# Three graph layers on one core: the first 112 nodes gathered edge by edge, or counted like all others

## The chip, the cores and the metric

The kernel runs on one core of a Trainium2 chip. The metric is the device time of one execution in microseconds (us), taken as the median of several runs. TensorE (PE) multiplies, VectorE (DVE) and ScalarE (ACT) work elementwise, GpSimd (POOL) does the same more slowly and issues transfers, SyncE (SP) only issues transfers.

## The reference

There are N = 2500 nodes with 256 numbers each and E = 80000 edges, sorted by destination. Three layers follow a normalization; a final product takes all four stages.

```python
h = jnp.maximum(_layernorm(x, axis=-1), 0.0)
def _edge_conv(x, src, dst, W, b):
    xi = x[dst]
    xj = x[src]
    m = jnp.concatenate([xi, xj - xi], axis=-1) @ W + b
    s = jax.ops.segment_sum(m, dst, num_segments=N)
    cnt = jax.ops.segment_sum(jnp.ones((dst.shape[0],), m.dtype), dst, num_segments=N)
    return s / jnp.maximum(cnt, 1.0)[:, None]
xs = [h]
for W, b in ((W0, b0), (W1, b1), (W2, b2)):
    h = jax.nn.relu(_edge_conv(h, src, dst, W, b))
    xs.append(h)
out = x + jnp.concatenate(xs, axis=-1) @ Wf + bf
```

A layer is linear before its Relu. With the halves Wt and Wb of W it is, up to the division by the in-degree, `cnt * h (Wt - Wb) + A (h Wb)`, where `A[d, s]` is the number of edges from s to d.

## The kernel before, in words

**Data.** The nodes are 20 tiles of 128 (`NT`, the last one with 68). `hT` holds the layer's input turned, features on the partitions and nodes in columns. `z` is `h Wb`, nodes on the partitions; it is split into two reduced-precision parts, `zh` and `zl`, so that two fast matmuls give the accuracy of one slow one.

**The count matrix.** Destinations are taken in windows of six nodes (`W`). For a window, up to 256 of its edges are fetched, and two one-hot tiles are made from source and destination by comparing on DVE (`compare`, which writes `one_m` and `one_n`); their product on PE (`counts`) is the window's part of the count matrix, which ACT takes out of the bank (`take_counts`). Four windows are a batch, 80 windows a group of 480 columns: groups 0 to 3 have 480, group 4 has 468. A group is a tile `a` of 20 source tiles by its columns.

**The first 112 nodes.** Windows begin at node 112 (`FEW`). The first 112 nodes have another way. `z` is kept in DRAM (`z_dram`: `keep_nodes` in layer 1, a store in `nodes_pair` later). For edge number e of each of these nodes, `gather` fetches the row of `z` of its source by an indirect transfer from POOL, 56 transfers a layer, eight of which fill eight slots of `sums` while the others add to them. `add_sums` adds the eight slots on DVE. `few_start` puts the own product of the 112 nodes into two PSUM banks on PE, and `few_end` adds the gathered sums by a product with `only`, a shifted identity, and takes the Relu.

**Layer 1** (`layer`, called for g = 0 to 4). For each group PE does 80 wide matmuls (20 source tiles, two output halves, `zh` and `zl`) and four own products, and in between, at seven points, the `counts` of the next group. `finish` completes a group (a row for the bias) and stores it to `a_dram` in bf16: POOL transfers that narrow on the way for groups 0 to 3; for group 4 `store_a` narrows on ACT and SP stores. On POOL's queue a part of the layer's gathers stands ahead of each store (`GATHERED`), and the five `add_x` transfers, which add x to the output, ahead of group 1's. What comes before the first group is an order written out by hand (`order`, a list of short names: C for `counts`, E for `take_counts`, B for `compare`, X and Y for the steps of `keep_nodes`, `ix` for `few_edges`).

**Layers 2 and 3.** `nodes_pair(l, t)` makes `z` for tiles t and t + 10, with their sums in `sh` and `sl`, and adds the previous layer's part of the final product (`final`). Then `Stream` runs the count matrix out of `a_dram`: `Alone` is group 4, by 80 wide matmuls; each `Pair` is two groups at once, by a scheme of seven products (`SEVEN`) in place of eight, 140 wide matmuls and seven own products. SP loads a chunk (`staged`, three buffers), ACT or DVE makes its `block`s five steps ahead (`LEAD`), PE multiplies. Since the gathers need all of `z` in DRAM, the work on the first nodes of the next layer is put late: the pair of tiles 0 and 10 comes after two steps of `Alone`, the chunk with tile 0 is the last one (`CHUNKS`), and the next layer's weights are loaded behind it. These lines set that order:

```python
        stream.run(tick, {0: [few_end], 2: [first_nodes], 12: [sums_of_w]})
    ts = [*range(1, 8), NT - 3, NT - 2, NT - 1, *range(8, NT - 3)]
```

All recorded instructions go through one helper, so the profile gives line 282 for nearly all of them; they are told apart by their tiles. The order on each engine is the program's own. At the end a flag (`missing`) says whether the counted edges are E; if they are not, a general version runs.

Of the kernel before, what the change touches and what calls it, by code (L numbers as in the profile page):

```python
# [313 lines left out]
def by_windows(ctx: ExitStack, tc: tile.TileContext, x, src, dst, Ws, bs, Wf, bf, out, missing):  # L314
# [17 lines left out]
    FEW = 112  # L332
    EDGES = 56
    SUMS = 8
    PAIRS = 4
    NW = (N - FEW) // W
# [3 lines left out]
    NONE = NP - 1  # L340
# [7 lines left out]
    while sum(GWS) < NW:  # L348
        GWS.append(min(80, NW - sum(GWS)))
    G = max(GWS) * W  # L350
    GS = 480
# [10 lines left out]
    assert E == P * R and FEW + NV == N and IN_LAST + FEW <= P and BW * NB <= 512 and G <= 512 and CAP <= 256  # L362
# [43 lines left out]
    z_dram = [dram.tile([NP, D], F32, name=f"z_dram{l}") for l in range(L)]  # L406
    who = const.tile([P, EDGES], I32, name="who")
    sums = const.tile([P, SUMS, D], F32, name="sums")
    only = const.tile([P, FEW], F32, name="only")
    cnt_few = const.tile([P, FEW], F32R, name="cnt_few")  # L410
    mine = const.tile([P, W], F32, name="mine")
    most = const.tile([P, 1], F32, name="most")
# [55 lines left out]
    POOLo.iota(lim_i[:, :WG - 1], pattern=[[P * W, WG - 1]], base=FEW, channel_multiplier=W)  # L468
    POOLo.iota(lim_i[:, WG - 1:], pattern=[[0, 1]], base=-IN_LAST, channel_multiplier=1)
    POOLo.iota(lim_i[:IN_LAST, WG - 1:], pattern=[[0, 1]], base=FEW + (WG - 1) * P * W, channel_multiplier=W)  # L470
    limr_i = pp.tile([P, WG * P], I32, name="limr_i")
    POOLo.iota(limr_i[:, :NW], pattern=[[W, NW]], base=FEW, channel_multiplier=0)
    POOLo.iota(limr_i[:, NW:], pattern=[[1, WG * P - NW]], base=0, channel_multiplier=0)
# [9 lines left out]
    def load_b(l, queue=SP):  # L483
# [8 lines left out]
    POOL.tensor_copy(only, ident[:, IN_LAST:IN_LAST + FEW])  # L492
    POOL.memset(cnt_few.bitcast(F32), 0.0)

    POOL.memset(mine, 0.0)
    POOL.affine_select(mine[:, 0:1], ones, pattern=[[0, 1]], compare_op=OP.is_ge, fill=0.0,
                       base=IN_LAST + FEW - 1, channel_multiplier=-1)
    POOL.memset(mine[:IN_LAST], 1.0)
    POOL.memset(most, float(EDGES))
    POOL.memset(most[:IN_LAST], float(CAP))  # L500
# [122 lines left out]
    def few_edges():  # L623

        es, ed = edges[WG - 1]
        own = pp.tile([P, EDGES], I32, name="own")
        POOLo.tensor_scalar(who, es[:, :EDGES], -NONE, None, op0=OP.add)
        POOLo.tensor_scalar(own, away[:, WG - 1, :EDGES], 1.0, None, op0=OP.is_equal)
        POOLo.tensor_tensor(who, who, own, op=OP.mult)
        POOLo.tensor_scalar(who, who, NONE, None, op0=OP.add)  # L630

# [28 lines left out]
    def degrees(i):  # L660
# [12 lines left out]
        for w0 in range(0, min(P, NW - i * P), P // 2):  # L673
            n = min(P // 2, NW - i * P - w0)
            pc = bank()
            for c in range(W):
                PEo.matmul(pc[:, :n * W].rearrange("p (w c) -> p w c", c=W)[:, :, c],
                          deg_b[:, i, c:c + 1].to_broadcast([P, P]), ident_b[:, w0:w0 + n], start=True, stop=True)
            to = FEW + (i * P + w0) * W
            ACTo.copy(cnt[:, to:to + n * W], pc[:, :n * W])  # L680
            yield
        if i == WG - 1:
            pc = bank()
            PEo.matmul(pc[:, :FEW], deg_b[:, i, 0:1].to_broadcast([P, P]), ident_b[:, IN_LAST:IN_LAST + FEW],
                       start=True, stop=True)
            ACTo.copy(cnt[:, :FEW], pc[:, :FEW])
            ACTo.copy(cnt_few[PAD:PAD + 1], cnt[PAD:PAD + 1, :FEW])
            yield

    def shares():  # L690
# [5 lines left out]
        last = deg[:, WG - 1, :]  # L696
        DVEo.scalar_tensor_tensor(last, last, most, mine, op0=OP.min, op1=OP.mult)
# [112 lines left out]
    def group_of(g):  # L810
        return FEW + sum(GWS[:g]) * W, GWS[g] * W
# [57 lines left out]
    def finish(g, a):  # L869
# [4 lines left out]
        gathered(GATHERED[g])  # L874
        if g == 1:
            for t in range(0, NT, 5):
                add_x(t, t + 5)
        store_a(g, a)
        yield

    def store_a(g, a):
        if g < alone:
            for t in range(0, NT, 5):
                POOLo.dma_start(a_dram[g][:, t:t + 5, :], a[:, t:t + 5, :].bitcast(F32))
            return
        short = new_a(g + 1).rearrange("p t n -> p (t n)").bitcast(BF16)[:, :NT * GS].rearrange(
            "p (t n) -> p t n", n=GS)
        for t in range(0, NT, 2):
            ACTo.copy(short[:, t:t + 2, :], a[:, t:t + 2, :].bitcast(F32))
        for t in range(0, NT, Q):  # L890
            SPo.dma_start(a_dram[g][:, t:t + Q, :], short[:, t:t + Q, :])

    def by_count(g):
        c0, n = group_of(g) if g < NG else (0, FEW)
# [3 lines left out]

    def keep_nodes(l, a, b):

        to = z_dram[l][a * P:b * P, :].rearrange("(q i p) d -> p i q d", i=2, p=P)
        ways = [(slice(0, 2), 0)] if b - a == 2 else [(i, slice(None)) for i in range(2)]

        def tiles_of(z):
            return z[:, :, a // 2 * D:b // 2 * D].bitcast(F32).rearrange("p i (q d) -> p i q d", d=D)

        for i, q in ways:
            SPo.dma_start(to[:, i, q, :], tiles_of(zh)[:, i, q, :])
        yield
        for i, q in ways:  # L910
            POOLo.dma_start(to[:, i, q, :], tiles_of(zl)[:, i, q, :], accum_op=OP.add)

    def gather(l):

        for e in range(EDGES):
            POOLo.indirect_dma_start(
                out=sums[:, e % SUMS, :], out_offset=None, in_=z_dram[l][:, :],
                in_offset=bass.IndirectOffsetOnAxis(ap=who[:, e:e + 1], axis=0),
                **({"compute_op": OP.add} if e >= SUMS else {}))
            yield  # L920

    first_gather = [None, 0]

    def gathered(n):
        if first_gather[0] is None:
            first_gather[0] = gather(0)
        while first_gather[1] < n:
            next(first_gather[0], None)
            first_gather[1] += 1

    few_banks = []

    def few_start(l):
        few_banks[:] = bank(), bank()
        for o, pa in enumerate(few_banks):
            for c in range(DC):
                PEo.matmul(pa[:, :FEW], ws[l][0][:, c, o * P:(o + 1) * P], hT[:, c, :FEW], start=(c == 0), stop=False)
            for z in (zh, zl):
                PEo.matmul(pa[:, :FEW], tile_of(z, NT - 1)[:, o * P:(o + 1) * P], cnt_few, start=False, stop=False)

    def add_sums():
        n = SUMS
        while n > 1:
            n //= 2
            DVEo.tensor_add(sums[:, :n, :], sums[:, :n, :], sums[:, n:2 * n, :])

    def few_end():
        for o, pa in enumerate(few_banks):
# [95 lines left out]
    for g in range(NG):  # L1044
# [12 lines left out]
        for u, _ in enumerate(layer(0, g, a, own, PEo, ACTo)):  # L1057
# [7 lines left out]
            if u == NT - 1 and g + 1 < NG:  # L1065
                run(extra)
                by_count(g + 1)
                if g == NG - 2:
                    by_count(NG)
# [319 lines left out]
```

## Time and profile before

| what | value |
|---|---|
| median of 3 runs | 520.09 us (519.41 to 520.48) |
| the profiled execution, its time | 520.36 us |
| its span, first to last instruction | 518.6 us |
| granted TensorE clock, mean | 0.962 |
| busy: PE, DVE, ACT, POOL | 478.4, 362.6, 244.8, 338.4 us |
| transfers | 82.42 MB, 159 GB/s |
| gathers (`sums<-z_dram,who`) | 168, 1672 ns each on POOL |

The span lies 1.76 us under the time of the same execution. Busy times of engines overlap. PE's busy time is modelled at the ends of matmuls, which are pipelined: a row of 0.37 us can be followed by the next one after 0.21 us, so steps are read from start to start. In rows of a timeline the columns are start, length, engine, line, operation, output and inputs with their shapes, count, and in brackets the idle time before it with what ended it.

### The profile page before, as it was taken

How to read it: one execution, taken by the hardware profiler on the slowest of the kernel's cores; microseconds unless marked ns; L12 is line 12 of the kernel's file. 1: busy time of each engine (PE TensorE's matmuls, PEld its weight loads, DVE VectorE, ACT ScalarE, POOL GpSimd, SP SyncE). 2: the span in 40 equal slices, each digit the busy share in tenths (PEclk: the TensorE clock that was granted, in tenths of full speed). 3: DMA queues.
4: the chain of work that ended last, by engine and by line, in shares of the span. 5: the costliest groups of instructions: out<-in, count | busy, mean ns of one | idle time of the engine just before them, and what ended most of it. 6: DMA issues, size and time to landing. Idle time of an engine off the chain costs nothing.

```text
span 518.6 us, 7749 instructions
## 1 busy us (share of the span) xinstructions
PE 478.4 (92%) x2787; PEld 393.0 (76%) x2787; DVE 362.6 (70%) x764; ACT 244.8 (47%) x458; POOL 338.4 (65%) x252
## 2 busy tenths in 40 slices
PE   8999999999999999989999999999599999999503
PEld 4878887788787887868888688788487877878402
DVE  7999889888988503586859688577534878865203
ACT  5667576846443543367454353357193444421000
POOL 4687338677888885000488888888007888888850
PEclk9999999999999999997999999999799999999856
DMA  9326995997988999933869887679377686846991
GB/s 292 123 83 121 184 218 147 185 210 108 181 132 149 134 191 164 194 119 106 293 172 212 200 197 144 116 129 168 57 213 258 144 228 118 197 60 123 159 79 49
DMA packets 60921, 82.42 MB, mean 159 GB/s; under 512 B 5337, under 2 KB 55978, under 8 KB 60586
## 3 DMA queue, kind: packets, MB, share of 16 engines
q0 software_dynamic: 30032, 38.62, 50.3%
q1 hardware_dynamic: 29914, 42.11, 25.7%
q10 hardware_dynamic: 928, 1.11, 0.7%
q8 instruction: 24, 0.39, 0.3%
q14 instruction: 23, 0.19, 0.1%
HBM read 56.48 MB, written 25.98 MB: 159 GB/s over the span
## 4 chain that ended last, share of the span: by engine, by line
POOL 37%; PE 34%; issue 11%; DMA 9%; DVE 6%; ACT 1%; SPq 0%; POOLq 0%; DVEq 0%; ACTq 0%
POOL sums L282 36%; PE bank L282 31%; DMA z_dram<-tmp 5%; PE pz L282 3%; DMA acc<-in_x_dram 1%; DMA sums<-z_dram,who 1%; DMA wb<-in_L_gnn_W_dram 1%; DVE sums L282 1%; DMA es<-in_src_dram,start_i 1%; DVE one_m L282 1%; DVE one_n L282 1%; POOL acc L282 1%; DVE tmp L282 1%; DVE zl L282 1%; ACT tmp L282 1%
## 5 line engine op out<-in xcount | busy, mean ns | idle before, releaser
L282 POOL DMA_INDIRECT sums<-z_dram,who x168 | 280.9, 1672 | 71.1 <-issue 47.5
L282 ACT CAST block<-staged 128x960 fp32r<-128x960 bf16 x80 | 74.5, 992 | 37.7 <-issue 22.7
L282 PE MATMUL bank<-block,zh 128*128 128x480 f32 (+1 forms) x200 | 84.1, 420 | 0.0
L282 PE MATMUL bank<-a,zh 128*128 128x480 f32 (+1 forms) x200 | 81.2, 406 | 0.0
L282 PE MATMUL bank<-block,zl 128*128 128x480 f32 (+1 forms) x200 | 77.8, 389 | 0.0
L282 DVE TENSOR_TENSOR one_m<-iota_m,key_m 128x1024 bf16<-128x1024 bf16 x100 | 68.5, 685 | 13.2 <-PE bank L282 12.3
L282 ACT CAST a<-bank 128x480 fp32r<-128x480 f32 x100 | 50.6, 566 | 55.2 <-PE bank L282 54.1
L282 PE MATMUL bank<-a,zl 128*128 128x480 f32 (+1 forms) x200 | 75.7, 378 | 0.0
L282 DVE TENSOR_TENSOR block<-block,staged 128x960 fp32r<-128x960 f32 x60 | 67.7, 1154 | 4.6 <-PE bank L282 1.7
L282 PE MATMUL bank<-block,sh 128*128 128x480 f32 x160 | 66.8, 417 | 0.0
L282 DVE TENSOR_TENSOR one_n<-iota_n,key_n 128x480 bf16<-128x480 bf16 x200 | 63.6, 357 | 0.0
L282 PE MATMUL bank<-block,sl 128*128 128x480 f32 x160 | 60.6, 379 | 0.0
L282 PE MATMUL bank<-wf,hT 128*128 128x256 f32 x240 | 56.7, 386 | 0.0
L282 PEld LDWEIGHTS bank<-wf,hT 128*128 128x128 f32 x240 | 46.4, 194 | 6.5
L282 PEld LDWEIGHTS bank<-block,zh 128*128 128x128 f32 x200 | 39.5, 198 | 8.4 <-issue 3.0
L282 PEld LDWEIGHTS bank<-block,zl 128*128 128x128 f32 x200 | 39.4, 197 | 8.3 <-issue 3.0
L282 PEld LDWEIGHTS <-one_m 128*128 128x128 bf16 x796 | 37.3, 98 | 9.0 <-issue 3.4
L282 PEld LDWEIGHTS bank<-a,zh 128*128 128x128 f32 x200 | 37.7, 188 | 8.2 <-issue 3.1
L282 PEld LDWEIGHTS bank<-a,zl 128*128 128x128 f32 x200 | 37.7, 188 | 6.9 <-issue 2.1
L282 PE MATMUL bank<-one_n,one_m 128*128 128x120 bf16 (+1 forms) x796 | 42.4, 208 | 0.1
L282 ACT ACTIVATE hT<-bank 128x480 f32<-128x480 f32 (+2 forms) x20 | 8.9, 482 | 65.3 <-PE bank L282 65.3
L282 POOL DMA_DIRECT2D z_dram<-tmp x2 | 1.6, 792 | 57.8 <-ACT tmp L282 57.8
(168 smaller groups left out, 706.8 us busy)
## 6 DMA issues: line engine op xcount, KB each, us to landing
staged<-a_dram SPq DMA_DIRECT2D x42, 480.0 KB, 5.7
a_dram<-a POOLq DMA_DIRECT2D x16, 600.0 KB, 12.5
z_dram<-tmp SPq DMA_DIRECT2D x18, 256.0 KB, 3.9
staged<-a_dram SPq DMA_DIRECT2D x16, 240.0 KB, 4.6
sums<-z_dram,who POOLq DMA_INDIRECT x168, 5.3
out_dram<-acc SPq DMA_DIRECT2D x19, 128.0 KB, 4.9
a_dram<-a SPq DMA_DIRECT2D x2, 1200.0 KB, 11.3
acc<-in_x_dram POOLq DMA_DIRECT2D x3, 640.0 KB, 9.7
```

The source lines that it names most:

```text
L282: return self.tc.keep_in_program_order(call(*args, **kwargs))
```

## The change

All nodes from 0 on go through windows: 417 windows (the last reaches two columns past node 2499), in groups of 84 windows or 504 columns, the last with 81 or 486. A group has 21 batches of four windows (the last group a final batch of one), where it had 20. `FEW` and all that served it is gone: the gathers, `who`, `sums`, the stores of `z` to DRAM, `few_start`, `add_sums`, `few_end`. Since no work waits for `z` in DRAM, the node pairs run in order (layer 3 begins with pair 6, then 0), all ahead of `Alone`, chunks are (0, 1), (2, 3) and so on, each loaded by two transfers, and the next layer's weights are loaded after the last node pair. Group 4 is stored by POOL like the others, and `add_x` follows the store of group 0. In the order by hand, one batch is added to group 0 (C20, E20, and B24 for the batch ahead). In the diff below, removed functions are cut to their first line, and small edits in setup are left out.

```diff
     SKIP = 2
-    FEW = 112
-    EDGES = 56
-    SUMS = 8
-    PAIRS = 4
-    NW = (N - FEW) // W
+    NW = -(-N // W)
     NV = NW * W
...
     IN_LAST = NW - (WG - 1) * P
-    NONE = NP - 1
     NB = NT * W
...
     while sum(GWS) < NW:
-        GWS.append(min(80, NW - sum(GWS)))
+        GWS.append(min(84, NW - sum(GWS)))
     G = max(GWS) * W
-    GS = 480
+    GS = G
     NG = len(GWS)
...
     const.tile([P, 16], F32, name="between")
-    z_dram = [dram.tile([NP, D], F32, name=f"z_dram{l}") for l in range(L)]
-    who = const.tile([P, EDGES], I32, name="who")
-    sums = const.tile([P, SUMS, D], F32, name="sums")
-    only = const.tile([P, FEW], F32, name="only")
-    cnt_few = const.tile([P, FEW], F32R, name="cnt_few")
-    mine = const.tile([P, W], F32, name="mine")
-    most = const.tile([P, 1], F32, name="most")
     pairs = [(0, 1), (2, 3)]
...
     POOL.tensor_copy(ident_b, ident)
-    POOL.tensor_copy(only, ident[:, IN_LAST:IN_LAST + FEW])
...
     warm = pp.tile([P, 1], F32, name="warm")
...
         parts[i] = [lo_i]
-    def few_edges():
...
                           deg_b[:, i, c:c + 1].to_broadcast([P, P]), ident_b[:, w0:w0 + n], start=True, stop=True)
-            to = FEW + (i * P + w0) * W
+            to = (i * P + w0) * W
             ACTo.copy(cnt[:, to:to + n * W], pc[:, :n * W])
-            yield
-        if i == WG - 1:
-            pc = bank()
-            PEo.matmul(pc[:, :FEW], deg_b[:, i, 0:1].to_broadcast([P, P]), ident_b[:, IN_LAST:IN_LAST + FEW],
-                       start=True, stop=True)
-            ACTo.copy(cnt[:, :FEW], pc[:, :FEW])
-            ACTo.copy(cnt_few[PAD:PAD + 1], cnt[PAD:PAD + 1, :FEW])
             yield
...
     def group_of(g):
-        return FEW + sum(GWS[:g]) * W, GWS[g] * W
+        return sum(GWS[:g]) * W, GWS[g] * W
...
         ACTo.copy(a[PAD:PAD + 1, NT - 1, :n], cnt[PAD:PAD + 1, c0:c0 + n])
-        gathered(GATHERED[g])
-        if g == 1:
+        for t in range(0, NT, 5):
+            POOLo.dma_start(a_dram[g][:, t:t + 5, :], a[:, t:t + 5, :].bitcast(F32))
+        if g == 0:
             for t in range(0, NT, 5):
                 add_x(t, t + 5)
-        store_a(g, a)
         yield
-    def store_a(g, a):
-        if g < alone:
-            for t in range(0, NT, 5):
-                POOLo.dma_start(a_dram[g][:, t:t + 5, :], a[:, t:t + 5, :].bitcast(F32))
-            return
-        short = new_a(g + 1).rearrange("p t n -> p (t n)").bitcast(BF16)[:, :NT * GS].rearrange(
-            "p (t n) -> p t n", n=GS)
-        for t in range(0, NT, 2):
-            ACTo.copy(short[:, t:t + 2, :], a[:, t:t + 2, :].bitcast(F32))
-        for t in range(0, NT, Q):
-            SPo.dma_start(a_dram[g][:, t:t + Q, :], short[:, t:t + Q, :])
     def by_count(g):
-        c0, n = group_of(g) if g < NG else (0, FEW)
+        c0, n = group_of(g)
         for o in range(DC):
...
-    def keep_nodes(l, a, b):
...
-    def gather(l):
...
-    def gathered(n):
...
-    def few_start(l):
...
-    def add_sums():
...
-    def few_end():
...
     a = new_a(0)
-    kept = [keep_nodes(0, i, j) for i, j in ((0, 4), (10, 16), (16, NT), (4, 8), (8, 10))]
     acts = {
...
         "se": lambda i: search(*((0, 1), (1, WG))[i]), "ge": get_edges,
-        "ix": few_edges, "ka": key_parts, "km": key_low, "kb": key_high, "kt": key_turn,
+        "ka": key_parts, "km": key_low, "kb": key_high, "kt": key_turn,
...
         k11 N8 L6 B4 E2 L5 C3 B5 C4 T8 E3 E4 C5 V9 R8 E5 ge3 ka2 H9 sc2 Z7 H7 F8 G7 B6 N3 N2 ka3 km2 T2 R2 km3
-        kb2 C6 T3 kb3 B7 L7 kt2 Z2 B8 B9 L9 X0 X1 E6 C7 k22 k12 kt3 H2 N4 ix Y0 Y1 E7 B10 k13 k23 Z8 L2 C8 T4 C9 E8
-        C10 H8 X2 E9
-        F9 B11 B12 C11 G8 E10 C12 R4 E12 E11 B13 F5 B14 C13 R3 B15 C14 E13 E14 L8 Y2 B16 Z3 G9 B17 C15 C16 H3 X3 E15
-        G5 B18 F3 C17 E16 C18 F4 E17 B19 C19 Z4 L3 Y3 G3 B20 E18 B21 F2 E19 B22 H4 X4 L4 Y4 G4 B23 G2 ws
+        kb2 C6 T3 kb3 B7 L7 kt2 Z2 B8 B9 L9 E6 C7 k22 k12 kt3 H2 N4 E7 B10 k13 k23 Z8 L2 C8 T4 C9 E8
+        C10 H8 E9
+        F9 B11 B12 C11 G8 E10 C12 R4 E12 E11 B13 F5 B14 C13 R3 B15 C14 E13 E14 L8 B16 Z3 G9 B17 C15 C16 H3 E15
+        G5 B18 F3 C17 E16 C18 F4 E17 B19 C19 Z4 L3 G3 B20 E18 C20 B21 F2 E19 B22 H4 E20 L4 G4 B23 G2 B24 ws
     """
...
     LATE = [NT] * 4
-    GATHERED = [0, 8, 21, 34, EDGES]
     extra = chain(degrees(0), finish(0, a), later_loads(), degrees(1))
...
                 by_count(g + 1)
-                if g == NG - 2:
-                    by_count(NG)
         run(extra)
...
                 ACTo.activation(zf[:, part], pz[:, part], AF.Copy, scale=share[:, u:u + 1])
-        (SPo if t else POOLo).dma_start(z_dram[l].rearrange("(h t p) d -> p h t d", h=2, p=P)[:, :, t, :],
-                      zf.rearrange("p (h d) -> p h d", h=2))
         ACTo.copy(both_of(zh, t), zf.rearrange("p (h d) -> p h d", h=2))
...
             st = stage.tile([P, 4, 2, GS], BF16, name="staged")
-            j0, j1 = CHUNKS[c]
-            for k, n in ((0, 2),) if j1 == j0 + 1 else ((0, 1), (1, 1)):
-                j = CHUNKS[c][k]
-                for i, g in enumerate(pairs[self.i]):
-                    SPo.dma_start(st[:, 2 * i:2 * i + 2, k:k + n, :],
-                                  a_dram[g].rearrange("p (h j) n -> p h j n", h=2)[:, :, j:j + n, :])
+            j = 2 * c
+            for i, g in enumerate(pairs[self.i]):
+                SPo.dma_start(st[:, 2 * i:2 * i + 2, :, :],
+                              a_dram[g].rearrange("p (h j) n -> p h j n", h=2)[:, :, j:j + 2, :])
             return st
...
             to = self.bank[what]
-            if c == len(CHUNKS) - 1:
+            if c == Q // 2 - 1:
                 if part[0] == "x":
...
                 PEo.matmul(to, w, self.r[what] if m is None else m, start=False, stop=False)
-            for k, j in enumerate(CHUNKS[c]):
+            for k, j in enumerate((2 * c, 2 * c + 1)):
                 for z in range(2):
...
                                          start=(c == 0 and k == 0 and z == 0),
-                                         stop=(c == len(CHUNKS) - 1 and k == 1 and z == 1))
+                                         stop=(c == Q // 2 - 1 and k == 1 and z == 1))
...
             n = self.n
-            if c == 1 and i == 0:
+            if c == 0 and i == 0:
                 self.banks = [bank(), bank()]
...
                         unit[0] = PEo.matmul(self.banks[o][:, :n], tile_of(z, t)[:, o * P:(o + 1) * P],
-                                             made[i][:, k, :n], start=(t == 4 and z is zh), stop=False)
-            if c == 0 and i == 1:
+                                             made[i][:, k, :n], start=(t == 0 and z is zh), stop=False)
+            if c == 4 and i == 1:
                 for o in range(DC):
...
         for p in Alone(l), Pair(l, 0), Pair(l, 1):
-            for c in range(5) if isinstance(p, Pair) else (1, 3, 4, 2, 0):
+            for c in range(5) if isinstance(p, Pair) else (0, 1, 3, 2, 4):
                 loads.append((p, c))
...
         stream.load(3)
-        order = [1, 2, 3, 4, 5, 6, 7, 8, 9] if l == 1 else [6, 7, 1, 2, 3, 4, 5, 8, 9]
-        for i, t in enumerate(order):
+        for i, t in enumerate(range(Q) if l == 1 else [6, 0, 1, 2, 3, 4, 5, 7, 8, 9]):
             nodes_pair(l, t)
-            if i == 0:
-                few_start(l - 1)
-            if i == 5:
+            if i == 6:
                 stream.make(2)
-            if i == 6:
-                add_sums()
-        def first_nodes():
-            nodes_pair(l, 0)
-            run(gather(l))
-            load_wf(l + 1, SPo)
-            if l + 1 < L:
-                load_b(l + 1, SPo)
-                load_wb(l + 1, SPo)
-                load_wt(l + 1, SPo)
+        load_wf(l + 1, SPo)
+        if l + 1 < L:
+            load_b(l + 1, SPo)
+            load_wb(l + 1, SPo)
+            load_wt(l + 1, SPo)
...
-        stream.run(tick, {0: [few_end], 2: [first_nodes], 12: [sums_of_w]})
+        stream.run(tick, {12: [sums_of_w]})
         if l + 1 < L:
...
-    ts = [*range(1, 8), NT - 3, NT - 2, NT - 1, *range(8, NT - 3)]
-    few_start(L - 1)
-    for i, t in enumerate(ts):
+    for t in [*range(7), NT - 4, NT - 3, NT - 2, NT - 1, *range(7, NT - 4)]:
         final(L, t)
-        if i == NT - 5:
-            add_sums()
-        if i == NT - 3:
-            few_end()
-    final(L, 0)
```

More of the change, by code (lines that the diff above doesn't have):

```diff
@@ L361, in by_windows @@
     assert NP <= 4096 and HR <= 512
-    assert E == P * R and FEW + NV == N and IN_LAST + FEW <= P and BW * NB <= 512 and G <= 512 and CAP <= 256
+    assert E == P * R and N <= NV <= NP and BW * NB <= 512 and G <= 512 and CAP <= 256
     assert E + P < 2 ** 24 and LAST <= PAD < P - 1 and D == DC * P
@@ L467, in by_windows @@
     lim_i = pp.tile([P, WG], I32, name="lim_i")
-    POOLo.iota(lim_i[:, :WG - 1], pattern=[[P * W, WG - 1]], base=FEW, channel_multiplier=W)
-    POOLo.iota(lim_i[:, WG - 1:], pattern=[[0, 1]], base=-IN_LAST, channel_multiplier=1)
-    POOLo.iota(lim_i[:IN_LAST, WG - 1:], pattern=[[0, 1]], base=FEW + (WG - 1) * P * W, channel_multiplier=W)
+    POOLo.iota(lim_i[:, :WG - 1], pattern=[[P * W, WG - 1]], base=0, channel_multiplier=W)
+    POOLo.iota(lim_i[:, WG - 1:], pattern=[[0, 1]], base=NP, channel_multiplier=0)
+    POOLo.iota(lim_i[:IN_LAST, WG - 1:], pattern=[[0, 1]], base=(WG - 1) * P * W, channel_multiplier=W)
     limr_i = pp.tile([P, WG * P], I32, name="limr_i")
-    POOLo.iota(limr_i[:, :NW], pattern=[[W, NW]], base=FEW, channel_multiplier=0)
-    POOLo.iota(limr_i[:, NW:], pattern=[[1, WG * P - NW]], base=0, channel_multiplier=0)
+    POOLo.iota(limr_i[:, :NW], pattern=[[W, NW]], base=0, channel_multiplier=0)
+    POOLo.iota(limr_i[:, NW:], pattern=[[0, WG * P - NW]], base=NP, channel_multiplier=0)
     row_i = pp.tile([P, MORE], I32, name="row_i")
@@ L491, in by_windows @@
     POOL.tensor_copy(ident_b, ident)
-    POOL.tensor_copy(only, ident[:, IN_LAST:IN_LAST + FEW])
[L493 to L500, printed above, removed]
     warm = pp.tile([P, 1], F32, name="warm")
@@ L621, in key_parts @@
         parts[i] = [lo_i]
-    def few_edges():
[L625 to L630, printed above, removed]
     def key_low(i):
@@ L694, in shares @@
         found = hot.tile([P, 1], F32, name="found")
-        last = deg[:, WG - 1, :]
-        DVEo.scalar_tensor_tensor(last, last, most, mine, op0=OP.min, op1=OP.mult)
         DVEo.reduce_sum(found, deg.rearrange("p i c -> p (i c)"), axis=mybir.AxisListType.X)
@@ L893, in by_count @@
     def by_count(g):
-        c0, n = group_of(g) if g < NG else (0, FEW)
+        c0, n = group_of(g)
         for o in range(DC):
             DVEo.tensor_mul(hT[:, o, c0:c0 + n], hT[:, o, c0:c0 + n], cnt[:, c0:c0 + n])
-    def keep_nodes(l, a, b):
[L901 to L911, printed above, removed]
@@ L913, in gather @@
-    def gather(l):
[L915 to L922, printed above, removed]
-    def gathered(n):
[L925 to L929, printed above, removed]
@@ L931, in by_windows @@
-    few_banks = []
-    def few_start(l):
[L934 to L939, printed above, removed]
-    def add_sums():
[L942 to L945, printed above, removed]
@@ L947, in few_end @@
-    def few_end():
-        for o, pa in enumerate(few_banks):
-            PEo.matmul(pa[:, :FEW], sums[:, 0, o * P:(o + 1) * P], only, start=False, stop=True)
-            ACTo.activation(hT[:, o, :FEW], pa[:, :FEW], AF.Relu)
     unit = [None]
@@ L1001, in by_windows @@
         "F": lambda q: product(q, wfs[0]), "G": first_final,
-        "X": lambda i: next(kept[i]), "Y": lambda i: next(kept[i], None),
         "B": compare, "C": counts, "E": lambda b: take_counts(b, a),
@@ L1092, in by_windows @@
         (("s", S2), "r2"), (("s", S3), "r3"), (("x", 1, 1), "r4")
-    CHUNKS = [(1, 2), (3, 4), (5, 6), (7, 8), (9, 0)]
     LEAD = 5
@@ L1300, in run @@
                     p.multiply(c, part, what, made)
-                    if c == len(CHUNKS) - 1:
+                    if c == Q // 2 - 1:
                         p.take(what)
```

## The prediction, made before the changed kernel ran

> **What bounds the kernel now.** I read the page's engine rows first, then its 40 slices, then a table of stretches cut at the borders between the layers, and last the waits and the order of time at the end.
>
> ```profile
> span 518.6 us, 7749 instructions
> PE 478.4 (92%) x2787; PEld 393.0 (76%) x2787; DVE 362.6 (70%) x764; ACT 244.8 (47%) x458; POOL 338.4 (65%) x252
> PE   8999999999999999989999999999599999999503
> ```
>
> TensorE is busy in nearly every slice; three places are not full: a mild one at the 18th (8), the 5 at about 363 to 376 us, and the last three (5, 0, 3). The stretches (PE busy and count, then PEld, DVE, ACT, POOL, clock, DMA) put numbers to it:
>
> ```profile
> 61.50:91.30 29.80, 29.80 (x274) 24.08 (x272) 26.16 (x69) 20.71 (x59) 15.69 (x17) 1.00 0.85 185
> 91.30:120.30 29.00, 29.00 (x261) 23.50 (x260) 25.79 (x67) 16.27 (x42) 20.43 (x16) 1.00 1.14 199
> 198.30:257.50 59.20, 56.33 (x257) 49.53 (x256) 39.96 (x80) 32.37 (x55) 10.24 (x8) 0.94 0.71 176
> 257.50:332.80 75.30, 75.30 (x317) 59.44 (x317) 57.88 (x65) 30.37 (x36) 64.33 (x37) 1.00 0.77 174
> 332.80:394.70 61.90, 55.87 (x257) 49.12 (x257) 37.39 (x79) 33.90 (x56) 32.06 (x22) 0.94 0.70 153
> 394.70:470.00 75.30, 75.30 (x317) 59.44 (x316) 56.65 (x63) 30.50 (x36) 64.64 (x36) 1.00 0.69 153
> 470.00:518.60 48.60, 21.22 (x97) 18.07 (x95) 12.50 (x24) 2.44 (x4) 26.56 (x18) 0.73 0.76 105
> ```
>
> In layer 1 (61.5 to 198.3) and in the two stretches of pairs PE never stops. It loses 2.9 us and 6.0 us at the two layer borders, and 27.4 us at the end. The waits say to whom:
>
> ```profile
> PE bank L282 <- DVE sums L282: 31.3, 3, 22.4
> DVE sums L282 <- DMA sums<-z_dram,who: 28.5, 2, 21.2
> DVE one_m L282 <- PE bank L282: 12.3, 14, 1.9
> ```
>
> All three PE waits (31.3 us) are for `sums`, the added gathers; two of them wait for the last gather itself. The end in order of time:
>
> ```profile
> 471.30 4.97 PE L282 MATMUL bank<-wf,hT 128*128 128x256 f32 x22
> 500.20 1.55 POOL L282 DMA_INDIRECT sums<-z_dram,who  x1 [0.30 <-issue]
> 507.01 2.41 DVE L282 TENSOR_TENSOR sums<-sums 128x1024 f32<-128x1024 f32 x3 [21.16 <-DMA sums<-z_dram,who]
> 509.48 1.20 PE L282 MATMUL bank<-only,sums 128*128 128x112 f32 x4 [22.42 <-DVE sums L282]
> 513.68 0.48 DVE L282 SCALAR_TENSOR_TENSOR acc<-bank,share,acc 128x256 f32<-128x256 f32 x1 [0.75 <-PE bank L282]
> ```
>
> PE has nothing more to do from 487.06 to 509.48. POOL issues 56 gathers per layer, about 1.85 us apart, so a layer's chain is over 100 us long and it starts only when the last node pair is in DRAM (389.09). So the kernel is bound by PE up to 487, and by POOL's chain of gathers after it.
>
> **The change part by part.** The sum is made against the profiled execution: span 518.6, time 520.36, so 1.76 us lie outside the span. The median of the three runs is 520.09, 0.27 less.
>
> *Removed at the end.* Now the stretch from 470.0 takes 48.6 us. Afterwards `few_start`, the wait, `add_sums` and `few_end` are gone. What stays: 20 products with Wf. A node pair's 16 matmul records (wb and wf, 128x256) start 3.45 us apart, so one tile and one weight take 0.863, and 20 take 17.3. Then 0.2 to the reader of the bank, 0.5 for the accumulation (the 0.48 row), and 4.9 from issue to landing (page, `out_dram<-acc`): 22.9. Saved: 25.7.
>
> *Removed at the borders.* From the first node pair to the last wide matmul of `Alone` it takes 59.2 and 61.9 us. The pure stream is 10 pairs x 3.454 = 34.5, and 80 matmuls of 468 columns x 0.2115 (mean step where nothing waits) = 16.9: 51.4. Saved: 7.8 and 10.5. In this lie few_start (1.28 each, 201.74 to 203.02), few_end (0.88 each), the two waits, and a slow clock behind each wait. One rule of the Trainium skill is weighed here (page "TensorE: Matmul & The Clock Gate", section "Part 1: The HAM clock gate"): the array falls to half clock after an idle window of about 3.4 us and is back after about 3.4 us of work. The trace differs:
>
> ```profile
> 233.74 1.20 PE L282 MATMUL bank<-only,sums 128*128 128x112 f32 x4 [2.87 <-DVE sums L282]
> 235.15 0.59 PE L282 MATMUL bank<-block,zl 128*128 128x468 f32 x1
> 235.54 0.59 PE L282 MATMUL bank<-block,zh 128*128 128x468 f32 x1
> ```
>
> A wait of 2.87 us was enough, and the 0.39 step lasted 6.1 us (until 239.83) and 4.9 us behind the second wait. The slow clock costs half of that, 3.0 and 2.5; by the page 1.7 each, 2.1 us less to save. I take the trace. It also prices any new wait: one of some 3 us costs about 3 more.
>
> Total removed: 25.7 + 7.8 + 10.5 = 44.0.
>
> *Added columns.* Groups have 504 (the last 486) columns instead of 480 (468). The mean step is 216.7 ns at 480 and 211.5 at 468, 0.433 ns a column. Layer 1 has 320 wide and 80 narrower matmuls, layers 2 and 3 together 560 and 160: 880 x 24 x 0.433 = 9.15, and 240 x 18 x 0.433 = 1.87: 11.0 us. That this line holds from 480 to 504 is assumed; lower end 0 (steps rounded up already), upper end a step kept in proportion to columns to the whole (216.7 x 24/480 = 10.8 ns), 11.4. The line is the nearest. The own products are full f32 (four took 3.14 us at 468, 195.15 to 198.29: 1.68 ns a column): 44 x 24 + 12 x 18 = 1272 columns, 2.1 us.
>
> *Added windows.* 417 instead of 398. A window's two matmuls take 0.089 us (16 records in 0.71): 19 x 0.089 = 1.7 us of PE; a batch of four more in each group. DVE compares cost 0.685 + 2 x 0.357 = 1.40 a batch, five batches 7.0 us; ACT takes five more banks out at 0.57. This I cost at nothing: in layer 1 a group gets 1.35 us longer on PE and 1.45 on DVE, and DVE waited 12.3 us for PE's banks, about 3 a group. Without that cover up to 7 us come onto the path.
>
> *Wider elements on DVE and ACT.* Per chunk of a pair DVE makes 4 blocks (1.154 us, with 5% 1.21) and ACT 3 (0.99, 1.04): 4.8 and 3.1 beside 28 x 0.227 = 6.4 of PE. Nothing. `by_count`, 10 x 5% of 0.65: nothing, behind the same slack.
>
> *Stores and loads.* The last group was narrowed by ACT (10 casts, 9.04 us, ended at 187.8) and stored by SP (2 x 11.3 to land). It becomes four POOL transfers from 178.8 on, each 1.59 to issue (at most 3.57) and 12.5 to land (at most 21.9), so about 198, or 215 at worst; `Alone` first casts from it at about 225. Here a rule speaks against the change (page "SBUF — State Buffer", section "SBUF: two separate sides"): a POOL transfer's descriptors can't be written while a DVE instruction in a two-port mode holds their shared port, its example going from 0.62 to 3.1 us. The trace has stores beside compares at the 12.5 already, and in 182 to 200 DVE is idle (0.00). By the rule, four times 2.5 more: landing 208 to 225, just under the cover; both sums are equal. Groups 1 to 3 no longer stand behind 8, 13 and 13 gathers on POOL. The five `add_x` transfers (7.0 us of POOL) move from behind group 1's gathers to behind group 0's store, about 77 to 84, before group 1's store at 92; they read ACT's copies, done at 62.4, and are used from 198. On SP the z stores go; next-layer weights are issued ahead of `Alone`'s fifth load and wait for the last node pair's products, and that load is needed some 14 us later: nothing. 480 KB loads become 504 KB, 5.7 to land against 6.4 a chunk with three buffers: nothing; cover gone, 5% of 5.7 per chunk.
>
> *Order of node pairs.* Layer 3 has pair 6 alone as cover before pair 0, which needs tile 10 from the last product's Relu. Before, that Relu ended 1.9 us after PE's last product (332.84 to 334.74); pair 6 covers 3.45. In layer 1 the extra batch adds to the head, in the 1.7.
>
> Sum: 518.6 - 44.0 + 11.0 + 2.1 + 1.7 = 489.4 span, with 1.76 outside 491.2, less 0.27 for the median: **491.0**.
>
> **The rivals.**
>
> *PE waits again at the borders (0.16).* Pair 0 and few_end gave ACT and DVE time to finish zh, zl and blocks. For it: DVE needs some 3.0 to 3.3 us per node pair against PE's 3.45. Against: in 344 to 362 both follow PE without falling behind, and the 16.02 us landing of a `z_dram<-tmp` store, which held the tmp buffers up to 217, goes. Price: 1 to 3 us of wait and as much slow clock, twice: 495 to 503, middle 497.
>
> *Better than the stream (0.06).* Head and tail gain from a lighter DMA (168 gathers on a queue at 50.3% of the 16 engines), and the column cost is nearer its lower end: 482 to 487, middle 485.5.
>
> *Slower: the wide matmul is not on the line (0.03).* Place: 880 matmuls at 504 columns. If a step lies above the line by more than (520.1 - 491.0) / 880 = 33 ns, so above 260 instead of 227, the gain is gone. At 270 it would be 529. Against: 468, 480 and the 256 of the other products show one slope near 0.43.
>
> *It doesn't do what it says (0.01).* If the counted edges were not all, the general branch would run, far slower; a window holds 256 edges. The largest window of six in these inputs has 241, and the most for a window's first two nodes is 89 of 128. A tie (0.01) needs several of these at once.
>
> **How the numbers follow.** Forecast 0.73, 488 to 495 alone; border waits 0.16; better 0.06; slower 0.04 together, tie 0.01. Within 0.2% is about what a measurement of this kernel can't tell from no change. Faster: 0.73 + 0.16 + 0.06 = 0.95. The range takes the forecast's own, most of the border waits and half of the better case: 485.5 to 499.
>
> **What would show it.** Right: no PE wait above 1 us at the borders, those stretches at 52 us each, the last at 23; clock 1.00 behind the borders; wide steps of 227 ns; layer 1 longer by 6 us and each stretch of pairs by 3.5; POOL nearly empty after 200. Wrong: a PE wait for `block` or `zl` at a border with 0.39 us steps behind it, DVE compares that PE waits for by more than 3 us in all, `staged` loads as a releaser, or steps above 240 ns.

## The result, and the profile after

The changed kernel takes **493.47 us** (median of 4 runs, 493.13 to 493.74), the kernel before 519.99 beside it on the same chip. The ratio is 0.949, with a 95% interval of 0.9474 to 0.9507: 26.5 us less. The forecast was 491.0, range 485.5 to 499, which is 29.1 less than the 520.09 it started from. In the experiments below, too, the ratio is to the kernel before beside the run; its medians there lie between 518.41 and 519.93. The profiled execution has a span of 491.9 us where the sum gave 489.4.

The page first: span and busy times, the slices of PE and of the granted clock, and the transfer queues.

```profile
span 491.9 us, 7411 instructions
PE 481.7 (98%) x2776; PEld 384.0 (78%) x2776; DVE 366.6 (75%) x767; ACT 241.3 (49%) x445; POOL 43.2 (9%) x66
...
PE   8999999999999999999999999999999999999994
...
PEclk9999999999999999999999999999999999999999
...
q1 hardware_dynamic: 19850, 33.54, 20.8%
q0 software_dynamic: 5856, 16.51, 17.6%
```

The three gaps of PE are gone, and the row of the clock has no dip. PE is busy 3.3 us longer in all than before (481.7 against 478.4): that small difference is what is left of two larger ones, more columns on one side, the slow clock and the products of the first nodes on the other. POOL, which was busy 65% of the span, has 9%.

The same cuts as before, now at layer 1, border, pairs, border, pairs, tail (PE busy and count, then PEld, DVE, ACT, POOL, granted clock, DMA share, GB/s):

```profile
61.30:205.00 143.70, 143.70 (x1173) 112.07 (x1172) 105.57 (x277) 68.20 (x170) 17.16 (x25) 1.00 0.61 119
205.00:257.20 52.20, 52.20 (x242) 45.48 (x241) 38.20 (x78) 33.16 (x53) 0.00 (x0) 1.00 0.34 115
257.20:336.40 79.20, 79.20 (x318) 59.41 (x317) 60.12 (x65) 31.73 (x36) 0.00 (x0) 1.00 0.35 112
336.40:388.60 52.20, 52.20 (x242) 45.47 (x241) 35.20 (x76) 34.42 (x54) 0.00 (x0) 1.00 0.25 85
388.60:467.60 79.00, 79.00 (x317) 59.44 (x316) 59.09 (x63) 31.69 (x36) 0.00 (x0) 1.00 0.28 92
467.60:491.90 24.30, 17.45 (x81) 15.01 (x79) 10.36 (x21) 1.98 (x2) 0.00 (x0) 0.95 0.34 109
```

In every stretch but the last PE's busy time equals the length, and the granted clock is 1.00: nothing is left to wait for, and no slow steps are left. From the first matmul of one stretch to the first of the next they compare like this:

| stretch | before | after | forecast of the difference | measured |
|---|---|---|---|---|
| layer 1 | 136.82 | 143.69 | +6 | +6.9 |
| border 1 | 59.24 | 52.18 | to about 52 | -7.1 |
| pairs, layer 2 | 75.31 | 79.23 | +3.5 | +3.9 |
| border 2 | 61.87 | 52.21 | to about 52 | -9.7 |
| pairs, layer 3 | 75.31 | 79.02 | +3.5 | +3.7 |
| tail | 48.6 (from 470.0) | 24.3 (from 467.6) | to 22.9 | -24.3 |

The longest waits of PE in the whole span lie in the start of the kernel, before layer 1, and the cover that the forecast leaned on is still there in layer 1:

```profile
PE bank L282 <- DVE idle L483: 1.5, 1, 1.5
PE turned L282 <- POOL acc L282: 0.6, 2, 0.4
PE bank L282 <- DVE pick L282: 0.4, 1, 0.4
...
DVE one_m L282 <- PE bank L282: 14.0, 21, 1.9
```

The last row is DVE waiting for PE's banks (12.3 us before), not the other way round: the compares of the five added batches did stay hidden.

### The profile page after: what moved, and what is told of

It reads as the page before. It is cut to its first block, busy times and chain, and to the rows that moved or that the text cites. A ratio compares the mean times of both kernels' runs of the same rounds, so it can differ in the third digit from the quotient of the medians.

```text
span 491.9 us, 7411 instructions
## 1 busy us (share of the span) xinstructions
PE 481.7 (98%) x2776; PEld 384.0 (78%) x2776; DVE 366.6 (75%) x767; ACT 241.3 (49%) x445; POOL 43.2 (9%) x66
## 2 busy tenths in 40 slices
DMA packets 26679, 51.73 MB, mean 105 GB/s; under 512 B 1945, under 2 KB 22378, under 8 KB 26602
## 4 chain that ended last, share of the span: by engine, by line
PE 91%; DVE 3%; POOL 3%; DMA 1%; issue 1%; SPq 0%; POOLq 0%
PE bank L282 87%; PE pz L282 3%; POOL acc L282 2%; DMA acc<-in_x_dram 1%; DVE st L282 1%; POOL ed L282 1%; POOL es L282 0%; DVE mv L282 0%; PE turned L282 0%; DVE zl L282 0%; DVE rs L282 0%; DVE off L282 0%; DVE away L282 0%; DVE one_m L282 0%; DVE kn L282 0%
## 5 line engine op out<-in xcount | busy, mean ns | idle before, releaser
L282 ACT CAST block<-staged 128x1008 fp32r<-128x1008 bf16 x80 | 77.6, 1031 | 40.9 <-issue 38.2
L282 PE MATMUL bank<-a,zh 128*128 128x504 f32 (+1 forms) x200 | 84.3, 422 | 0.0
L282 PE MATMUL bank<-block,zh 128*128 128x504 f32 (+1 forms) x200 | 83.4, 417 | 0.0
L282 DVE TENSOR_TENSOR one_m<-iota_m,key_m 128x1024 bf16<-128x1024 bf16 (+1 forms) x105 | 72.0, 686 | 14.1 <-PE bank L282 14.0
L282 PE MATMUL bank<-a,zl 128*128 128x504 f32 (+1 forms) x200 | 77.8, 389 | 0.0
L282 PE MATMUL bank<-block,zl 128*128 128x504 f32 (+1 forms) x200 | 77.6, 388 | 0.0
L282 DVE TENSOR_TENSOR block<-block,staged 128x1008 fp32r<-128x1008 f32 x60 | 70.8, 1205 | 4.9 <-PE bank L282 1.7
L282 PE MATMUL bank<-block,sh 128*128 128x504 f32 x160 | 68.7, 429 | 0.0
L282 DVE TENSOR_TENSOR one_n<-iota_n,key_n 128x480 bf16<-128x480 bf16 (+1 forms) x210 | 66.9, 359 | 0.0
L282 PE MATMUL bank<-block,sl 128*128 128x504 f32 x160 | 62.5, 391 | 0.0
```

The source lines that it names most:

```text
L282: return self.tc.keep_in_program_order(call(*args, **kwargs))
```

## The experiments

**The price of the columns.** The kernel after with 398 windows in groups of 80, as many as before; the edges of the last 112 nodes are left out. Small edits in setup and the order by hand without its added batch are not shown.

```diff
-    NW = -(-N // W)
+    NW = 398
...
-        GWS.append(min(84, NW - sum(GWS)))
+        GWS.append(min(80, NW - sum(GWS)))
```

> The changed kernel with 398 windows in groups of 80 (480 columns, the last 468), so that the last 112 nodes get no sums at all: left out are their windows and their layer outputs. It is the change without its price. Theory A, the price is columns and windows only: layer 1 shorter by some 7 us, each border by 0.8, each stretch of pairs by 3.9, together 16.2, about 477.3 us. Theory B, part of the growth is something else that came with the change (order of pairs, stores on POOL): the drop is smaller than 14.8, above 478.7 us.

Measured: 477.93 us, ratio 0.9211 [0.919, 0.9233]. So columns and windows cost 15.5 us (493.47 - 477.93), where the forecast had 11.0 + 2.1 + 1.7 = 14.8: theory A, since the drop is not smaller than 14.8. By the profiled spans the rest of the change brought 518.6 - 476.1 = 42.5 us, against 44.0 forecast.

**Is the wide step on a line?** The kernel after with 410 windows in groups of 82, 492 columns; the last 40 nodes are left out of the count matrix. Small edits in setup are not shown.

```diff
-    NW = -(-N // W)
+    NW = 410
...
-        GWS.append(min(84, NW - sum(GWS)))
+        GWS.append(min(82, NW - sum(GWS)))
```

> The kernel after with 410 windows in groups of 82, so 492 columns a group; the last 40 nodes are left out of the count matrix. Theory A (the wide step is a line in the columns, steeper by a little than the forecast's: 0.48 ns a column between 480 and 504): steps of 222.5 to 223, the time half way between the runs at 480 and 504 columns, 485.2 to 486. Theory B (the step jumps somewhere above 480 columns): steps near 217.5 or near 228, the time near 478.5 or near 492.5 less the windows, 491.

Measured: 487.95 us, steps of 223.2 ns. Mean steps from start to start, where neighbours are alike, stand at 217.2 ns (480 columns, kernel before), 223.2 (492) and 228.6 (504): close to one line, of 0.48 ns a column, no jump. At the same width such a mean moves by up to 1 ns from one program to the next (217.2 to 218.2 at 480 columns). The "half way" in the expectation was an error of arithmetic: 410 windows are 12/19 of the way from 398 to 417, which gives 477.93 + 0.63 x 15.54 = 487.7, and 487.95 agrees with that. Theory A holds for the step; its time as written missed. The timelines show the step as the difference of neighbouring starts, first the kernel after, then the one with 480 columns:

```profile
299.98 0.39 PE L282 MATMUL bank<-block,zl 128*128 128x504 f32 x1
300.21 0.39 PE L282 MATMUL bank<-block,sh 128*128 128x504 f32 x1
300.44 0.39 PE L282 MATMUL bank<-block,sl 128*128 128x504 f32 x1
```

```profile
299.87 0.38 PE L282 MATMUL bank<-block,sh 128*128 128x480 f32 x1
300.08 0.38 PE L282 MATMUL bank<-block,sl 128*128 128x480 f32 x1
300.30 0.38 PE L282 MATMUL bank<-block,sh 128*128 128x480 f32 x1
```

**Row pitch.** The step of 228.6 ns is 1.5 above the 227.1 to which the forecast's line leads. A possible reason is where rows of 504 lie in SBUF. The kernel after with tiles `a` and `block` at a pitch of 512.

```diff
+    PITCH = 512
...
-        return apools[g % 2].tile([P, NT, GS], F32R, name="a")
+        return apools[g % 2].tile([P, NT, PITCH], F32R, name="a")[:, :, :GS]
```

> The changed kernel, but the rows of the count tiles in SBUF (the group tile a and the blocks) stand 512 elements apart instead of 504; widths and work are the same. In the trace of the changed kernel a wide step takes 228.1 ns at 504 columns and 220.9 at 486[...]. Theory A: the 1.5 ns more come from row pitch 504, so steps fall to 226.7 and 219.0, 1120 steps give 1.7 us, about 491.8 us. Theory B: they belong to the width; steps and time stay at 228.1 and 493.5.

Measured: 493.41 us, 0.9505 [0.9487, 0.9524]. No difference (theory B): the pitch is not the reason.

**Are the gathers the whole of the removed waits?** The kernel before with only eight gathers a layer, one for each slot of `sums`; the other edges of the first 112 nodes are left out.

```diff
-        for e in range(EDGES):
+        for e in range(SUMS):
```

> The kernel before with 8 gathers a layer instead of 56, so that most edges of the first 112 nodes are left out; few_start, add_sums, few_end and the stores of z stay. Theory A: all three PE waits hang on the gathers; they vanish with the slow clock behind them, 44.0 less three times 2.2 us for the small products: some 37.5 us less, about 482.5 us. Theory B: only the waits at the end and at the second border do; the first (2.87 us) comes from DVE that fell behind when a store of z took 16 us to land, and stays with its slow clock: about 488 us.

Measured: 483.81 us, 0.9322 [0.93, 0.9345], near theory A and not B. All that PE still waits for `sums` is one wait, the whole answer on PE's waits from layer 1 on:

```profile
PE bank L282 <- DVE sums L282: 1.2, 1, 1.2
```

The waits of both borders and of the end are gone together, although few_start, add_sums, few_end, the stores of `z` and the late node pair all stay. The borders take 53.5 us each, 1.9 more than the 51.66 of the kernel after with 480 columns: about what few_start and few_end cost on PE.

**Eight gathers fewer.** In these inputs none of the first 112 nodes has more than 47 edges, so 48 gathers hold them all; with more, `missing` would call the general version, as it does before with more than 56.

```diff
-    EDGES = 56
+    EDGES = 48
```

> The kernel before with 48 gathers a layer instead of 56 (these inputs have at most 47 edges for one of the first 112 nodes, so nothing is left out). Theory A: the end waits for the chain of gathers, 1.85 us each: 8 fewer take 14.8 off the end, and the 6 us wait at the second border goes with 2.5 of slow clock: about 497 us. Theory B: the chain is bound by transfers that land late rather than by the number issued; then the end shrinks by less than 8 us, above 505 us.

Measured: **493.14 us**, 0.9501 [0.9477, 0.9524]: for these inputs a change of one number is worth as much as the whole change. It brought more than the 497 that was expected. What PE still waits for `sums` says why:

```profile
PE bank L282 <- DVE sums L282: 8.2, 1, 8.2
```

Of the three waits for `sums` (31.3 us) only the last is left. It shrank from 22.4 to 8.2, 14.2 us for eight gathers: 1.8 each, near the 1.85 between two gathers. Both borders' waits vanish altogether, the first one too, and the slow clock behind them: the borders went from 59.24 and 61.87 to 53.59 each, 5.65 and 8.28 less. The waits were 2.87 and 6.03, so the slow clock had cost 2.8 and 2.3 us beside them. A chain that is a few us late costs its lateness and such a sum on top, and a small cut takes both away.

**Use the sums later.** The kernel with 48 gathers, with node pair 0 ahead of `Alone` so that the chain starts sooner, few_end inside the node pairs, and at the end one product later.

```diff
+            if i == 7:
+                few_end()
...
-        stream.run(tick, {0: [few_end], 2: [first_nodes], 12: [sums_of_w]})
+        first_nodes()
+        stream.run(tick, {12: [sums_of_w]})
...
-        if i == NT - 3:
+        if i == NT - 2:
```

> The kernel before with 48 gathers a layer, few_end ahead of the last two node pairs and the pair of tiles 0 and 10 as the last node pair ahead of Alone instead of after two of its steps, so that the gathers start some 3.5 us earlier; at the end few_end stands one product later. Nothing is left out. With 48 gathers alone PE still waited 8.2 us for sums at the end. Theory A: the chain of gathers sets the end; the wait falls by 3.5 and 0.9 us, with less slow clock: about 488 us. Theory B: what remains of the wait is fixed latency of the last gathers and of add_sums: the time stays near 493.

Measured: 496.41 us, 0.957 [0.9537, 0.9604], slower than the kernel with 48 gathers it starts from. Its last wait did go (0.31 us left), but the borders waited 2.0 us each for `sums`, since few_end came one node pair behind add_sums, and layer 1 took 144.03 us instead of 137.30, where nothing had been edited. The two waits at the borders are alike, but what follows them is not:

```profile
236.51 0.70 PE L282 MATMUL bank<-only,sums 128*128 128x112 f32 x4 [2.01 <-DVE sums L282]
237.04 1.91 PE L282 MATMUL bank<-wb,hT 128*128 128x256 f32 x8
...
367.55 0.85 PE L282 MATMUL bank<-only,sums 128*128 128x112 f32 x4 [2.00 <-DVE sums L282]
368.20 3.47 PE L282 MATMUL bank<-wb,hT 128*128 128x256 f32 x8
```

Behind the first wait the clock stayed at 1.00; behind the second it was at 0.50 from 367.95 to 371.35, and that border took 1.7 us longer than the first. So a wait of 2.0 us may bring the slow clock or not.

It was tried once more with add_sums one node pair sooner and a part of `Alone`'s blocks made one later (here against the run just told):

```diff
-            if i == 5:
+            if i == 6:
                 stream.make(2)
-            if i == 6:
+            if i == 5:
                 add_sums()
```

> The kernel before with 48 gathers a layer, node pair 0 ahead of Alone and the last few_end one product from the end, as in the earlier run of this kind, but few_end two node pairs later than add_sums has been issued (add_sums after the sixth node pair, few_end after the eighth). Theory A (only the last wait costs; the stall of 6.7 us in layer 1 of the earlier run belongs to that program's layout and does not come back): 493.1 less the 8 us of the tail wait, so 485 to 488, layer 1 at 137. Theory B (the stall comes with this order of node pairs): layer 1 again at 144 with waits put down to issue, 494 to 497. Theory C (moving node pair 0 ahead of Alone makes PE wait for its casts): layer 1 at 137, borders at 56 or more, 490 to 493.

Measured: **490.34 us** (6 runs, 489.59 to 491.44), 0.9443 [0.9414, 0.9473]: the fastest version that leaves nothing out, though the stall in layer 1 came back (142.98 us). The time lies in theory C's range, but its mechanism is out: the borders took 53.8. A's gain came (behind the last wide matmul 25.3 us are left, against 34.8 with 48 gathers alone), and B's stall came too. Its waits and the stall (PE, timeline; the bracket is the idle time before the row):

```profile
PE bank L282 <- issue: 2.4, 5, 0.5
...
PE bank L282 <- DVE sums L282: 0.3, 1, 0.3
```

```profile
85.77 0.25 PE L282 MATMUL bank<-one_n,one_m 128*128 128x120 bf16 x2 [0.54 <-issue]
86.49 0.21 PE L282 MATMUL bank<-one_n,one_m 128*128 128x120 bf16 x1 [0.48 <-issue]
87.20 0.30 PE L282 MATMUL bank<-one_n,one_m 128*128 128x80 bf16 x3 [0.49 <-issue]
...
91.40 0.60 PE L282 MATMUL bank<-a,zh 128*128 128x480 f32 x1
91.80 0.60 PE L282 MATMUL bank<-a,zl 128*128 128x480 f32 x1
```

Rows come 0.72 us apart with one to five matmuls each, and behind them the wide steps are 0.40 apart, at a granted clock of 0.50 from 89.4 to 92.75. The rows of PE, DVE, ACT and POOL in layer 1 are the same instructions in the same order as in the kernel with 48 gathers, which has none of these waits on PE. The cause is open. That instructions arrive late beside full DMA engines is only argued, and no run takes layer 1's gathers away from this place.

**Stores of `z` alone.** The kernel after with the stores of `z` to DRAM put back for layers 2 and 3, read by nothing.

```diff
+        SPo.dma_start(z_dram[l].rearrange("(h t p) d -> p h t d", h=2, p=P)[:, :, t, :],
+                      zf.rearrange("p (h d) -> p h d", h=2))
```

> The changed kernel with the stores of z to DRAM put back into nodes_pair on SP (nothing reads them), without gathers. Before, the first border had a PE wait of 2.87 us behind a store of z that took 16 us to land; with 48 gathers it was gone. Theory A: the gathers that were still running made the store late; without gathers the stores land in 2 to 5 us and cost nothing: 493.5 us. Theory B: the stores themselves hold the tmp buffers: a wait of 1 to 3 us at a border with slow clock behind, 496 us or more.

Measured: 493.32 us, 0.951 [0.9476, 0.9545]. The stores cost nothing (theory A): in the trace no engine waits for one. The 16 us that such a store took to land before had gathers beside it. That these made it late fits, but the trace of this run gives no landing to set beside it.

**Who narrows the last group.** The kernel after with group 4 narrowed by ACT and stored by SP, as before.

```diff
+        if g == alone:
+            for t in range(0, NT, 2):
+                ACTo.copy(short[:, t:t + 2, :], a[:, t:t + 2, :].bitcast(F32))
...
```

> The changed kernel with group 4 narrowed by ten casts on ACT and stored by SP again, as before. The prediction held this edit for free on either queue: 493.5 us, within 0.5. Rival: ACT's 9 us of casts or the later landing delay the first blocks of Alone and PE waits at the first border: 495 us or more.

Measured: 492.73 us, 0.95 [0.9467, 0.9533]; on PE no wait from layer 1 on. Either way is free. No gain is shown either: the profiled span is 1.0 us shorter, but 1.5 us of difference lie behind the last DVE row (4.8 us against 6.3), of which more below. After, the POOL transfers of `a` land in 7.5 us at the median, not the 12.5 that the forecast took.

```profile
a_dram<-a POOLq DMA_DIRECT2D x20, 630.0 KB, 7.5
```

**The order of node pairs.** The kernel after with layer 3 starting with pair 0, which needs the last tiles of the layer before.

```diff
-        for i, t in enumerate(range(Q) if l == 1 else [6, 0, 1, 2, 3, 4, 5, 7, 8, 9]):
+        for i, t in enumerate(range(Q) if l == 1 else [0, 1, 2, 3, 4, 5, 6, 7, 8, 9]):
```

> The changed kernel with node pair 0 first at the second border instead of pair 6. Tile 10 of pair 0 needs the last Relu of the layer, so PE waits for it. The prediction costed pair 6 as a cover of 3.45 us over a latency of 1.9. Theory A: PE waits some 1.9 us and its clock stays up, since the idle time is short: about 495.4 us. Theory B: the wait also brings the slow clock (a wait of 2.87 us did), up to 3 us more: about 498 us. Rival: no wait, 493.5.

Measured: 493.85 us, 0.9534 [0.9498, 0.9571], below what either theory gave and near the rival's 493.5, though not for its reason. The wait comes, but only 0.99 us long, since half of the pair's first products are for tile 0, which is ready:

```profile
336.43 1.02 PE L282 MATMUL bank<-wb,hT 128*128 128x256 f32 x4
338.44 1.13 PE L282 MATMUL bank<-wb,hT 128*128 128x256 f32 x4 [0.99 <-ACT hT L282]
339.41 1.89 PE L282 MATMUL bank<-wf,hT 128*128 128x256 f32 x8
```

Four records still take 0.97 behind it (338.44 to 339.41), eight 1.72 (339.41 to 341.13): there is no slow clock to speak of. The border is 1.26 us longer. The time is only 0.4 longer, within the interval, and the profiled span not at all, since its end came out 1.4 us shorter.

**The last stores.** The kernel after with the stores of `out` on SP's queue and ACT's in turn.

```diff
-                SPo.dma_start(out[t * P:t * P + n, :], acc[:n, t, :])
+                (SPo, ACTo)[t % 2].dma_start(out[t * P:t * P + n, :], acc[:n, t, :])
```

> The kernel after, with the stores of the output tiles alternating between SP's queue and ACT's instead of all on SP's. Theory A (the 6.3 us from the last DVE row to the end of the span are one transfer's own landing and the end of the program): 493.3, within 0.3. Theory B (the last store stands behind the stores before it on SP's queue): the span ends 1 to 1.5 us sooner, 492.

Measured: 492.74 us, 0.9483 [0.9454, 0.9511]. Its profiled span ends 5.7 us behind the last DVE row, against 6.3 after. But six other profiled executions, of kernels whose end is the one of the kernel after, end 4.8 to 5.9 behind it. No gain is shown, and one of half a us is not excluded.

**What stands behind the last row.** Here are the rows for landings of `out_dram<-acc`, first of the kernel before, then of the kernel after with 480 columns, and below them the end of the kernel after by stretches (columns as above), the first of which has the last DVE row:

```profile
DMA to landing us min/median/max: 4.1/4.9/6.4
...
DMA to landing us min/median/max: 1.7/1.9/3.4
```

```profile
485.00:485.57 0.57, 0.05 (x1) 0.00 (x0) 0.48 (x1) 0.00 (x0) 0.00 (x0) 1.00 0.34 115
...
486.50:487.00 0.50, 0.00 (x0) 0.00 (x0) 0.00 (x0) 0.00 (x0) 0.00 (x0) 1.00 0.93 273
487.00:487.50 0.50, 0.00 (x0) 0.00 (x0) 0.00 (x0) 0.00 (x0) 0.00 (x0) 1.00 0.06 16
487.50:488.00 0.50, 0.00 (x0) 0.00 (x0) 0.00 (x0) 0.00 (x0) 0.00 (x0) 1.00 0.00 0
488.00:489.00 1.00, 0.00 (x0) 0.00 (x0) 0.00 (x0) 0.00 (x0) 0.00 (x0) 1.00 0.04 6
```

By the packets of the trace all of the last store but eight packets is through 1.4 us behind that DVE row. These eight, of 1 KB each, end at 3.55, and the span ends 2.8 us behind them. In the six other executions they end at 2.0 to 3.2, and the span 2.6 to 2.9 us behind them. In all seven they end 0.7 us behind the end of a 16 KB fetch of instructions, so they seem to stand behind it; no run separates the two.

## Why the prediction was right, and by how much not

- **The tail** was the largest term: 25.7 us saved, where 24.3 came. PE's 20 products with Wf were right, 17.4 us against 17.3. What stands behind PE was mis-sized and mis-built: 6.85 us (485.05 to 491.9) against 0.2 + 0.5 + 4.9 = 5.6. The 4.9 was the landing of stores that had gathers beside them. Without a long chain of gathers such stores land in 1.7 to 3.7 us where traces tell it, and about 2.8 us of the program's end follow the last packets. That 4.9 came near what the other executions show, 4.8 to 5.9 behind the last DVE row, is luck; the 6.3 of this one is the longest of the seven. Before, the same end took 4.4.
- **The borders** were forecast at 52 and took 52.18 and 52.21. The pure stream of ten node pairs and 80 wide matmuls is therefore the whole of a border now. The kernel with eight gathers shows that all three waits belonged to the gathers. The slow clock was rightly counted as a cost of its own, at 3.0 and 2.5 us by the trace; the run with 48 gathers has 2.8 and 2.3. By the 3.4 us of the Trainium skill (page "TensorE: Matmul & The Clock Gate", section "Part 1: The HAM clock gate") it would be 1.7 each, an estimate, and 2.1 less saved. As a sum, the two borders shrank by 7.06 + 9.66 = 16.7 with the wider columns in them, and those cost about 0.75 a border (80 steps x 9.4 ns; the own products stand behind this cut), so 18.2 without, against 18.3 forecast.
- **The columns** were the other term that was mis-sized. The line from 468 to 480 gave 0.433 ns a column; the runs have 0.475 from 480 to 504, and 0.52 from 468 to 486. 880 x 11.4 + 240 x 9.4 ns = 12.3 us against 11.0. The shape of the step was right: the run at 492 lies on the line, so the rival "not on the line" is excluded, as is "steps rounded up already". A slope read from two sizes 12 columns apart, at steps known to about one ns, was too little to extend over 24 more: with 217.2 in place of 216.7 at 480 columns the same line has 0.475. The 11.4 that the prediction gave as the upper end of this term was too low.
- **Costed at nothing** were the compares, the wider blocks, POOL's stores, the moved additions of x, the loads and the new order of pairs. PE has no wait longer than 0.4 us from layer 1 on, so none of them came onto the path. The rule of the Trainium skill (page "SBUF — State Buffer", section "SBUF: two separate sides") that DVE can hold up a POOL transfer's descriptors decided nothing here: POOL's transfers of `a` landed in 7.5 us at the median, and PE has no wait with POOL nor, for group 4, with ACT and SP.
- **The rivals.** Border waits (0.16) did not come. "Better than the stream" (0.06) counted on a gain from a lighter DMA; transfers fell from 82.42 to 51.73 MB and gave no such gain.
- **The sum** missed by 2.5 us of span: 1.4 in the tail, 0.8 in layer 1 and 0.7 in pairs and borders, most of these two from the columns. The start gives some of it back: with one batch more it was 0.2 us shorter (61.47 to 61.28), where 0.4 more had been counted.

What the prediction did not see: the cheaper way to the same time. The 22.4 us at the end did not ask for the removal of 56 gathers, only for a chain that ends 22 us sooner. With these inputs eight fewer, an earlier start and a later use brought 490.34, while the change pays 15.5 us of PE to be rid of a chain that runs on another engine. Leaving the stall aside, that way would stand near 490.34 - (142.98 - 137.3) = 484.7, an estimate.

## What to carry to other kernels

Work on an idle engine is free up to its deadline and then costs its lateness at once. Here the slow clock came on top, 2.8 us behind a wait of 2.87 and 2.3 behind one of 6.03. So ask first by how much the chain is late and how early it could start, and only then what it would cost to move its work to the engine that bounds the kernel. Where that engine had been full everywhere else, the borders without their waits came out within 0.1 us of the sum of pure steps (51.4, and 0.75 for the wider columns). Read slopes from sizes that lie as far apart as the step to be taken. Read the end of a program from its last computing row to the end of the span, over several executions, and not from the landing of one transfer in other company.

## What the runs showed of the hardware

- Waits of PE of 0.99 and 1.2 us left no slow steps behind them. Of two waits of 2.0 us one left none, the other 3.4 us at a granted clock of 0.50. Waits of 2.87 and 6.03 us left slow steps for 6.1 and 5.0 us, and six gaps of 0.42 to 0.68 us within 5 us brought them too.
- The step of a wide matmul is 217.2, 223.2 and 228.6 ns at 480, 492 and 504 columns, and 228.4 at 504 with a row pitch of 512 in SBUF.
- The last eight packets of the last store ended 0.7 us behind a 16 KB fetch of instructions in seven executions, 2.0 to 3.6 us behind the last DVE row; the store's other packets were through by 1.4 to 1.7 us.
- The same instructions in the same order in layer 1 took 137.3 us in one program and 143 to 144 in two others that differ from it only later, with waits put down to issue on PE. All timed executions of each of the two lie within 1.9 us (489.59 to 491.44, and 495.75 to 496.50), so by their times it comes with the program; why is open.
